# Single rows of an embedding table fetched by two engines in turns, more gathers taken from GpSimd, and a later load of table parts

## The chip, the cores and the metric

The kernel runs on one core of a Trainium2 chip. The metric is the device time of one execution in microseconds (us). The profile is of one execution, and its span is the time between its first and its last recorded instruction.

## The reference

`r_seq` is 1024 x 50 item numbers, `table` 100001 rows of 128 float32, of which row 0 counts as zero.

```python
e = emb_table.at[0].set(0.0)[seq]                 # 1024 x 50 x 128
prefix = jnp.cumsum(e, axis=1)
denom = jnp.minimum(t_idx, lengths)               # t_idx = 1..50
uF = prefix / denom
y = (uF - uF.mean(0)) * rsqrt(uF.var(0) + 1e-5) * gamma + beta   # over the batch, for each step
# for each of the 50 steps, with v = 0 at first:
v = v + (x - v) / 2.0
spike = v >= 1.0
v = v - spike * 1.0
# mean of the spikes over the steps, times the whole table
scores = spikes.mean(0) @ emb.T                   # 1024 x 100001 float32, 409.6 MB
```

## The kernel before

The order of instructions on each engine is that in which the code emits them. Tiles hold the 128 features on the partitions and the 1024 sequences in the columns.

**First stage, a loop over t = 0 to 49.** `gather(t)` fetches the rows of step t into a tile `e` (two buffers): GpSimd (POOL in the profile) issues up to eight indirect DMAs of 128 rows each (line 247). TensorE (PE) transposes the eight blocks and adds them to the running sums `pre0` and `pre1` (line 390), ahead of which `correct` (line 348) takes row 0 out. VectorE (DVE) scales the sums to `uF` (line 401) and takes mean and variance, `bs` and `mv` (lines 402 and 410). ScalarE (ACT) makes the root `r` (line 414), centres `uF` (line 421), scales it to `v` (line 444) and takes `d = v - 1` (line 360); between these VectorE makes the small factors `q` and `a` and the new `v`. `gather(t + 2)` stands behind the transposes of step t, because it writes into the buffer that they read. So GpSimd may be up to two steps ahead of TensorE.

**Rows fetched one by one.** For the eight steps in `BY_SYNC`, GpSimd gathers only seven blocks. The eighth comes from `held_rows`, a tile of four slots of 128 columns. Its 128 rows are fetched one by one by SyncE (SP) in `fetch_singles`: four times a load of 32 byte addresses into registers (line 265) and 32 DMAs of one row of 512 bytes (line 268). The first 128 rows are emitted ahead of the loop, the next 128 at step 11 behind its transposes, and so on.

**Table parts.** SyncE first loads the beginning of the table, 38 parts of 0.5 MB (`fetch`, line 147): four small loads or groups for the first parts, and `AHEAD - 1` = 5 whole groups of six parts (3072 KB each). At step 44 one more load of two parts follows (line 473).

**Second stage.** The counts of spikes are multiplied with the table, part by part (transposes and products on TensorE, lines 176 and 200; copies by VectorE and ScalarE, lines 601 and 603), and SyncE stores the scores (line 209).

**Completion semaphores.** The DMAs of SyncE and ScalarE take eight completion semaphores in turn, in the order of the code, and each DMA waits until the earlier one on its semaphore has landed.

Of the kernel before, what the change touches and what calls it, by code (L numbers as in the profile page):

```python
# [17 lines left out]
U8 = mybir.dt.uint8  # L18
# [3 lines left out]
P = 128  # L22
# [4 lines left out]
BANK = 512  # L27
GROUP = 6
AHEAD = 6
# [3 lines left out]
SHIFT = TWICE + ASIDE  # L33
FURTHER = {5: 1, 6: 2}

BY_SYNC = (11, 17, 22, 28, 33, 38, 43, 48)
AT_ONCE = 32

SPARED = 120
PICKED = range(42, 97, 3)  # L40
# [7 lines left out]
def rec_kernel(  # L48
# [9 lines left out]
    nc = tc.nc  # L58
    B, T = seq.shape
    N, D = table.shape  # L60
    NB = B // P
# [16 lines left out]
    held_rows = const.tile([P, BANK], F32, tag="countB", name="held_rows")  # L78
# [16 lines left out]
    def pair(i):  # L95
        free.append([embp.tile([P, HALF], F32R, tag=f"{x}{i}", name=f"{x}_{i}") for x in ("hi", "lo")])

    def size(q):
        return min(HALF, N - q * HALF)
# [4 lines left out]
    def group(g):  # L104
        at = g if g < AHEAD else AHEAD - 2 + g % 2
        r = rowp.tile([P, GROUP, HALF], F32, tag=f"rows{at}", name=f"rows_{g}")
        for k in range(GROUP):
            rows[g * GROUP + SHIFT + k if g else k + ASIDE * (k >= TWICE)] = r[:, k, :]
        return r
# [19 lines left out]
    def pick(r, q, engine):  # L129
        j = PICKED.index(q)  # L130
        rows_of(r[:SPARED, :], picks, j)
        if j % 2:
            engine.dma_start(out=r[SPARED:, :], in_=runs[q * P + SPARED : (q + 1) * P, :])
            turn_by(TURN)
        else:
            turn_by(4)
            rows_of(r[SPARED:, :], ends, j // 2)
            turn_by(5)

    def fetch(r, k, q, n):  # L140

        engine = nc.sync if q < held else nc.scalar
        n = min(n, parts - q)
        whole = n - (size(q + n - 1) < HALF)
        wide = whole - (whole == n and q + whole - 1 in PICKED)
        if wide:
            engine.dma_start(
                out=r[:, k : k + wide, :],
                in_=table[q * HALF : (q + wide) * HALF, :].rearrange("(q p k) d -> p q (k d)", p=P, k=KQ),
            )  # L150
        if wide < whole:
            pick(r[:, k + wide, :], q + wide, engine)
        if whole < n:
            full, rest = divmod(size(parts - 1), KQ)
            c1 = (parts - 1) * HALF
            r = r[:, k + whole, :]
            if rest:
                at = full - full % 32
                nc.vector.memset(r[at : at + 32, :], 0.0)
                engine.dma_start(  # L160
                    out=r[full : full + 1, : rest * D],
                    in_=table[c1 + full * KQ : N, :].rearrange("(o k) d -> o (k d)", o=1),
                )
            if full:
                engine.dma_start(
                    out=r[:full, :],
                    in_=table[c1 : c1 + full * KQ, :].rearrange("(p k) d -> p (k d)", k=KQ),
                )
# [19 lines left out]
    def prepare(q, pt):  # L188
        turned(q, pt)
        split[q] = hi, lo = free.pop(0)  # L190
        vp, vh, vl = views(q, pt, hi, lo)
        nc.scalar.copy(vh, vp)  # L192
        nc.vector.tensor_tensor(vl, vp, vh.bitcast(F32), ALU.subtract)  # L193
# [18 lines left out]
    with ExitStack() as ph:  # L212
# [21 lines left out]
            rows[TWICE + k] = spare[:, k, :]  # L234
        fetch(spare, 0, TWICE, ASIDE)
        fetch(first, TWICE, SHIFT, GROUP - TWICE)
        for g in range(1, AHEAD):
            fetch(group(g), 0, g * GROUP + SHIFT, GROUP)


# [2 lines left out]

        def gather(t):
            es[t] = gp.tile([P, B], F32, tag="e", name=f"e_{t}")
            for n in range(NB - (t in BY_SYNC)):
                nc.gpsimd.indirect_dma_start(  # L247
                    out=es[t][:, n * P : (n + 1) * P],
                    out_offset=None,
                    in_=table,  # L250
                    in_offset=bass.IndirectOffsetOnAxis(ap=idx[:, n, t : t + 1].bitcast(U32), axis=0),
                )

        byte_rows = table.rearrange("n d -> (n d)").bitcast(U8)
        row_bytes = 4 * D
        starts = ids[:T, :P].bitcast(I32)
        regs = [nc.sync.alloc_register(f"row{k}") for k in range(AT_ONCE)]
        singles = {}

        def fetch_singles(i):  # L260
            t = BY_SYNC[i]
            rows_of = held_rows[:, i % (BANK // P) * P :][:, :P]
            singles[t] = rows_of
            for p0 in range(0, P, AT_ONCE):
                nc.sync.load(regs, starts[t : t + 1, p0 : p0 + AT_ONCE])  # L265
                for k, reg in enumerate(regs):
                    at = nc.sync.snap(reg, donate=True, min_val=0, max_val=(N - 1) * row_bytes)
                    nc.sync.dma_start(  # L268
                        out=rows_of[p0 + k : p0 + k + 1, :].bitcast(U8),
                        in_=byte_rows[bass.ds(at, row_bytes)].rearrange("(o b) -> o b", o=1),  # L270
                    )

        make_identity(nc, ident)
        isz = up.tile([P, NB, P], F32, tag="uF", name="isz")
        rb = up.tile([P, NB, P], F32, tag="uF", name="rb")
        gather(0)

        last_ids = ids[:, P : P + T]
        nc.vector.tensor_copy(last_ids, idx[:, NB - 1, :])
        ips = vp.tile([P, B], F32, tag="v0", name="ips")  # L280
        nc.tensor.transpose(ips[:T, :P], last_ids, ident)
        nc.vector.tensor_scalar_mul(starts, ips[:T, :P], float(row_bytes))
        fetch_singles(0)

        nc.vector.memset(isz, 0.0)
        for u in (0, P // 2):
# [46 lines left out]
        def only(t):  # L333

            k = t % ONLY
            if k == 0:
                n = min(ONLY, T - t)
                nc.vector.tensor_tensor(
                    ls[:, :n, :],
                    r0n.unsqueeze(1).to_broadcast([P, n, D]),  # L340
                    sel[:, t : t + n].unsqueeze(2).to_broadcast([P, n, D]),
                    ALU.mult,
                )
            return ls[:, k, :]
# [12 lines left out]
        def over(t, v):  # L357

            d = lp.tile([P, B], BF16, tag="d", name=f"d_{t}")
            nc.scalar.activation(d, v, AF.Identity, bias=less)  # L360
            return d
# [4 lines left out]
        def spiked(out, cs, v):  # L366
            nc.vector.scalar_tensor_tensor(out, v, V_TH, count[:, cs], ALU.is_ge, ALU.add)
# [12 lines left out]
        correct(0, only(0))  # L380
        l = only(1)
        gather(1)
        for t in range(T):
            last = t == T - 1
# [17 lines left out]
                nc.vector.bn_stats(bs[:, h, :], uF[:, cs])  # L402
            if t + 2 < T:
                gather(t + 2)
            if t in BY_SYNC[:-1]:
                fetch_singles(BY_SYNC.index(t) + 1)
            if not last:
                correct(t + 1, l)
            mv = sp.tile([P, 2], F32, tag="mv", name=f"mv_{t}")
# [33 lines left out]
            def x(vt, cs):  # L443
                nc.scalar.activation(vt, uF[:, cs], AF.Identity, bias=hgb[:, 1:2], scale=a)

            def step(vt, cs):
                nc.vector.scalar_tensor_tensor(vt, negv[:, cs], -0.5, vt, ALU.mult, ALU.add)  # L447

            if not last:
                vt = vp.tile([P, B], F32, tag=f"v{(t + 1) % 2}", name=f"v_{t}")  # L450
                x(vt, whole)
                if t:
                    spiked(count, whole, v)
                step(vt, whole)
                v = vt
                if t == T - 2:
                    spiked(count, whole, v)
                    moved = once.tile([P, P], F32, tag="r0hi", name="moved")
                    nc.vector.tensor_scalar_add(moved, v[:, pieceA], beta2)
                    near = once.tile([P, P], F32, tag="r0", name="near")  # L460
                    nc.vector.scalar_tensor_tensor(near, v[:, pieceA], V_TH, moved, ALU.is_ge, ALU.subtract)
                d = over(t, v)
                if t + 2 < T:
                    l = only(t + 2)

                if t in (T - 8, T - 6):
                    q = (t - T + 8) // 2
                    pair(q)
                    prepare(q, vp.tile([P, HALF], F32, tag="v0", name=f"pt_{q}"))
                    if q == TWICE - 1:  # L470
                        for k in range(TWICE):
                            rows[GROUP + ASIDE + k] = first[:, k, :]
                        nc.sync.dma_start(
                            out=first[:, :TWICE, :],
                            in_=table[(GROUP + ASIDE) * HALF : (GROUP + SHIFT) * HALF, :].rearrange(
                                "(q p k) d -> p q (k d)", p=P, k=KQ
                            ),
                        )

# [64 lines left out]
    for c, W in enumerate(WIDTHS):  # L546
# [38 lines left out]
        for n, q in blockwise:  # L585
# [4 lines left out]
            o = os[n]  # L590
# [27 lines left out]
            if n in (1, 4) and c >= MIDDLE and to_fetch < parts:  # L618
                g, k = divmod(to_fetch - SHIFT, GROUP)
# [26 lines left out]
```

## Time and profile before

| | us |
|---|---|
| three runs | 1845.76, 1851.0, 1854.84 |
| median | 1851.0 |
| profiled execution, its time | 1852.0 |
| its span | 1850.0 |
| first store of scores issued, from the start of the span | 802.8 |
| `r` of steps 0, 1, 2 and 3 | 22.5, 31.1, 49.2, 62.1 |
| `r` of steps 10 and 11 | 140.6, 178.8 |
| `r` of steps 48 and 49 | 789.0, 798.2 |

The mean granted clock of TensorE is 0.763. Over the span PE is busy for 58%, DVE 51%, ACT 36% and POOL 23%, and DMAs move 264 GB/s. These are means over two stages that differ: up to 802.8 us the 50 steps, behind it the products and stores. The times of `r` show how the steps go: most are short, and those in `BY_SYNC`, as step 11, take 30 to 50 us.

### The profile page before, as it was taken

How to read it: one execution, taken by the hardware profiler on the slowest of the kernel's cores; microseconds unless marked ns; L12 is line 12 of the kernel's file. 1: busy time of each engine (PE TensorE's matmuls, PEld its weight loads, DVE VectorE, ACT ScalarE, POOL GpSimd, SP SyncE). 2: the span in 40 equal slices, each digit the busy share in tenths (PEclk: the TensorE clock that was granted, in tenths of full speed). 3: DMA queues.
4: the chain of work that ended last, by engine and by line, in shares of the span. 5: the costliest groups of instructions: out<-in, count | busy, mean ns of one | idle time of the engine just before them, and what ended most of it. 6: DMA issues, size and time to landing. Idle time of an engine off the chain costs nothing.

```text
span 1850.0 us, 14486 instructions
## 1 busy us (share of the span) xinstructions
PE 1070.6 (58%) x4465; PEld 810.4 (44%) x4465; DVE 947.7 (51%) x1128; ACT 674.2 (36%) x698; POOL 429.7 (23%) x459
## 2 busy tenths in 40 slices
PE   3321302120212213088998988878888878888984
PEld 2110201010101112066676766666666666666763
DVE  4653707261524346175566655555555555555652
ACT  2331303130312123054555544444444444444542
POOL 6664716262716254200000000010010010000000
PEclk7555555555555555589999999999889899989998
DMA  9511101010201011069999999999999999999999
GB/s 351 178 44 28 49 15 46 21 48 16 50 14 45 17 41 32 15 266 413 405 422 402 431 421 426 425 427 428 426 427 427 426 427 428 423 422 429 427 428 391
DMA packets 54993, 488.27 MB, mean 264 GB/s; under 512 B 12719, under 2 KB 14000, under 8 KB 33796
## 3 DMA queue, kind: packets, MB, share of 16 engines
q1 hardware_dynamic: 32944, 431.39, 55.4%
q0 software_dynamic: 16560, 35.40, 6.6%
q10 hardware_dynamic: 5412, 20.56, 2.7%
q8 instruction: 35, 0.57, 0.1%
q14 instruction: 42, 0.34, 0.1%
HBM read 77.69 MB, written 409.60 MB: 263 GB/s over the span
## 4 chain that ended last, share of the span: by engine, by line
DMA 33%; PE 15%; DVE 4%; ACT 3%; SPq 3%; issue 3%; ACTq 0%; DVEq 0%
DMA scores<-o 33%; PE po L200 15%; DVE o L601 2%; ACT o L603 2%; SPq L268 2%; DVE pairs L193 1%; ACT pairs L192 1%; PE pt L176 0%; SPq L265 0%; ACT hi L192 0%; DVE lo L193 0%; DVE bs L402 0%; DVE uF L401 0%; DMA held_rows<-in_L_rec_emb_table 0%; ACTq L603 0%
## 5 line engine op out<-in xcount | busy, mean ns | idle before, releaser
L601 DVE TENSOR_SCALAR o<-po 128x1024 f32<-128x1024 f32 (+1 forms) x390 | 467.2, 1214 | 309.6 <-DMA scores<-o 163.7
L603 ACT ACTIVATE o<-po 128x1024 f32<-128x1024 f32 x392 | 393.2, 1025 | 490.7 <-DMA scores<-o 337.2
L247 POOL DMA_INDIRECT e<-in_L_rec_emb_table,idx x392 | 372.9, 951 | 377.2 <-PE pre L390 218.6
L200 PE MATMUL po<-pairs,countB 128*128 128x512 f32 (+1 forms) x1120 | 289.9, 404 | 47.8 <-ACT o L603 47.6
L200 PE MATMUL po<-pairs,countC 128*128 128x512 f32 (+1 forms) x840 | 243.9, 438 | 62.3 <-ACT o L603 55.4
L401 DVE SCALAR_TENSOR_TENSOR uF<-rlen,pre 128x512 f32<-128x512 f32 x100 | 67.9, 679 | 399.0 <-PE pre L390 317.2
L200 PEld LDWEIGHTS po<-pairs,countB 128*128 128x128 f32 x1120 | 208.3, 191 | 110.9 <-ACT o L603 64.9
L200 PEld LDWEIGHTS po<-pairs,countC 128*128 128x128 f32 x840 | 169.8, 210 | 115.9 <-ACT o L603 66.0
L348 PE MATMUL pre<-zT,ls 128*128 128x512 f32 x100 | 78.5, 787 | 227.3 <-DVE uF L401 136.7
L390 PE MATMUL pre<-ident,held_rows 128*128 128x128 f32 x8 | 3.6, 447 | 349.2 <-DMA held_rows<-in_L_rec_emb_table 349.2
L414 ACT ACTIVATE r<-mv,eps 128x1 f32<-128x1 f32 x50 | 14.8, 295 | 509.2 <-DVE mv L410 406.3
L122 POOL DMA_INDIRECT rows<-in_L_rec_emb_table,picks x19 | 18.6, 981 | 685.2 <-PE pt L176 681.9
L390 PEld LDWEIGHTS pre<-ident,held_rows 128*128 128x128 f32 x8 | 1.5, 183 | 351.7 <-issue 351.7
L348 PEld LDWEIGHTS pre<-zT,ls 128*128 128x128 f32 x100 | 29.4, 295 | 267.4 <-DVE uF L401 159.3
L193 DVE TENSOR_TENSOR pairs<-pt,pairs 128x1024 fp32r<-128x1024 f32 x70 | 85.3, 1218 | 98.0 <-ACT pairs L192 97.1
L390 PE MATMUL pre<-ident,e 128*128 128x128 f32 x392 | 101.3, 422 | 19.2 <-DMA e<-in_L_rec_emb_table,idx 12.7
L176 PE MATMUL pt<-ident,rows 128*128 128x128 f32 (+1 forms) x768 | 104.9, 282 | 9.3 <-DVE v L447 5.0
L176 PEld LDWEIGHTS pt<-ident,rows 128*128 128x128 f32 (+1 forms) x768 | 94.3, 147 | 26.3 <-issue 10.8
L390 PEld LDWEIGHTS pre<-ident,e 128*128 128x128 f32 x392 | 81.6, 219 | 37.4 <-DMA e<-in_L_rec_emb_table,idx 18.9
L200 PE MATMUL po<-hi,countB 128*128 128x512 f32 x208 | 84.8, 408 | 10.8 <-ACT o L603 9.2
L192 ACT CAST pairs<-pt 128x1024 fp32r<-128x1024 f32 x70 | 70.0, 1012 | 39.2 <-PE pt L176 39.2
L200 PE MATMUL po<-lo,countB 128*128 128x512 f32 x208 | 83.3, 401 | 0.0
(99 smaller groups left out, 1110.1 us busy)
## 6 DMA issues: line engine op xcount, KB each, us to landing
scores<-o SPq DMA_DIRECT2D x96, 3072.0 KB
scores<-o SPq DMA_DIRECT2D x32, 1536.0 KB
scores<-o SPq DMA_DIRECT2D x29, 1024.0 KB
scores<-o SPq DMA_DIRECT2D x8, 2896.5 KB
rows<-in_L_rec_emb_table ACTq DMA_DIRECT2D x19, 1024.0 KB
held_rows<-in_L_rec_emb_table SPq DMA_DIRECT2D x1024, 0.5 KB
rows<-in_L_rec_emb_table SPq DMA_DIRECT2D x5, 3072.0 KB
e<-in_L_rec_emb_table,idx POOLq DMA_INDIRECT x392
```

The source lines that it names most:

```text
L122: nc.gpsimd.indirect_dma_start(out=r, out_offset=None, in_=runs, in_offset=bass.IndirectOffsetOnAxis(ap=which[: r.shape[0], j : j + 1].bit ...
L176: nc.tensor.transpose(pt[:, k0 : k0 + pw], r[:pw, k0 : k0 + D], ident[:pw, :pw])
L192: nc.scalar.copy(vh, vp)
L193: nc.vector.tensor_tensor(vl, vp, vh.bitcast(F32), ALU.subtract)
L200: nc.tensor.matmul(po[:, :kw], lhsT=counts[n], rhs=part[:, k0 : k0 + kw], start=j == 0, stop=j == 1,)
L247: nc.gpsimd.indirect_dma_start(out=es[t][:, n * P : (n + 1) * P], out_offset=None, in_=table, in_offset=bass.IndirectOffsetOnAxis(ap=idx[: ...
L268: nc.sync.dma_start(out=rows_of[p0 + k : p0 + k + 1, :].bitcast(U8), in_=byte_rows[bass.ds(at, row_bytes)].rearrange("(o b) -> o b", o=1),)
L348: nc.tensor.matmul(pre[h], lhsT=l, rhs=zT[:, h * BANK : (h + 1) * BANK], start=t == 0, stop=False, skip_group_check=True,)
L390: nc.tensor.matmul(pre[h][:, k : k + P], lhsT=singles[t] if h * BANK + k + P == B and t in singles else e[:, h * BANK + k : h * BANK + k + P],
L401: nc.vector.scalar_tensor_tensor(uF[:, cs], rlen[:, cs], 1.0 / (t + 1), pre[h], ALU.max, ALU.mult)
L601: nc.vector.tensor_scalar_mul(o[:, h0 : h0 + hw], po[:, :hw], 1.0 / T)
L603: nc.scalar.mul(o[:, h0 : h0 + hw], po[:, :hw], 1.0 / T)
```

## The change

The single rows now serve eleven steps, `APART` = 7, 11, 15, ..., 47, instead of eight. They are fetched in 44 portions of 32 rows. A portion is emitted at the end of each step from `STARTED` = 1 on, so in steps 1 to 44: SyncE loads 22 addresses and fetches 22 rows, ScalarE loads 10 and fetches 10, the two emitted in turns (SyncE, ScalarE, SyncE, ...) until ScalarE has its ten. Of the groups of table parts that SyncE loaded first, those from `EARLY` = 2 on (four groups) are loaded behind the last portion. In the changed file the loads of addresses are lines 274 and 275, the single rows 265, gathers 249, table parts 149, `r` 421, `uF` 428, `v` 451, `d` 369, the reload 480 and the stores 211.

```diff
-BY_SYNC = (11, 17, 22, 28, 33, 38, 43, 48)
-AT_ONCE = 32
+APART = tuple(range(7, 48, 4))
+STARTED = 1
+SYNC_ROWS, OWN_ROWS = 22, 10
+EARLY = 2
...
-        for g in range(1, AHEAD):
+        for g in range(1, EARLY):
             fetch(group(g), 0, g * GROUP + SHIFT, GROUP)
...
-            for n in range(NB - (t in BY_SYNC)):
+            for n in range(NB - (t in APART)):
                 nc.gpsimd.indirect_dma_start(
...
-        regs = [nc.sync.alloc_register(f"row{k}") for k in range(AT_ONCE)]
+        sync_regs = [nc.sync.alloc_register(f"row{k}") for k in range(SYNC_ROWS)]
+        own_regs = [nc.scalar.alloc_register(f"own{k}") for k in range(OWN_ROWS)]
...
-        def fetch_singles(i):
...
+        def fetch_row(engine, reg, row):
+            at = engine.snap(reg, donate=True, min_val=0, max_val=(N - 1) * row_bytes)
+            engine.dma_start(
+                out=row.bitcast(U8),
+                in_=byte_rows[bass.ds(at, row_bytes)].rearrange("(o b) -> o b", o=1),
+            )
+
+        def fetch_some(i, p0):
+            t = APART[i]
+            rows_of = singles[t] = held_rows[:, i % (BANK // P) * P :][:, :P]
+            p1 = p0 + SYNC_ROWS
+            nc.sync.load(sync_regs, starts[t : t + 1, p0:p1])
+            nc.scalar.load(own_regs, starts[t : t + 1, p1 : p1 + OWN_ROWS])
+            for k, reg in enumerate(sync_regs):
+                fetch_row(nc.sync, reg, rows_of[p0 + k : p0 + k + 1, :])
+                if k < OWN_ROWS:
+                    fetch_row(nc.scalar, own_regs[k], rows_of[p1 + k : p1 + k + 1, :])
+
+        todo = [(i, p0) for i in range(len(APART)) for p0 in range(0, P, SYNC_ROWS + OWN_ROWS)]
...
-        fetch_singles(0)
...
-            if t in BY_SYNC[:-1]:
-                fetch_singles(BY_SYNC.index(t) + 1)
...
+                if t >= STARTED and todo:
+                    fetch_some(*todo.pop(0))
+                    if not todo:
+                        for g in range(EARLY, AHEAD):
+                            fetch(group(g), 0, g * GROUP + SHIFT, GROUP)
```

In the order of instructions a row names the line, the operation, and the tile written and read. `rows` and `spare` are table parts, `ids` the byte addresses, `held_rows` the single rows. SyncE's opening was this before:

```order
L147 DMA rows_106<-in_L_rec_emb_table 128x4x1024
L147 DMA rows_111<-in_L_rec_emb_table 128x6x1024
L147 DMA rows_113<-in_L_rec_emb_table 128x6x1024
L147 DMA rows_115<-in_L_rec_emb_table 128x6x1024
L147 DMA rows_117<-in_L_rec_emb_table 128x6x1024
L147 DMA rows_119<-in_L_rec_emb_table 128x6x1024
L265 TENSOR_LOAD ids
L268 DMA held_rows<-in_L_rec_emb_table 1x512 x32
```

And it is this with the change:

```order
L149 DMA rows_106<-in_L_rec_emb_table 128x2x1024
L149 DMA spare<-in_L_rec_emb_table 128x2x1024
L149 DMA rows_106<-in_L_rec_emb_table 128x4x1024
L149 DMA rows_111<-in_L_rec_emb_table 128x6x1024
L274 TENSOR_LOAD ids
L265 DMA held_rows<-in_L_rec_emb_table 1x512 x22
```

The single rows now stand behind one group instead of five, and go in portions of 22. The end of SyncE's first stage, with the first store (`scores`), was this before:

```order
L265 TENSOR_LOAD ids
L268 DMA held_rows<-in_L_rec_emb_table 1x512 x32
L473 DMA rows_106<-in_L_rec_emb_table 128x2x1024
L209 DMA scores<-o_0_3455 128x512 x2
L209 DMA scores<-o_1_3456 128x512 x2
```

And with the change:

```order
L480 DMA rows_106<-in_L_rec_emb_table 128x2x1024
L274 TENSOR_LOAD ids
L265 DMA held_rows<-in_L_rec_emb_table 1x512 x22
L149 DMA rows_3652<-in_L_rec_emb_table 128x6x1024
L149 DMA rows_3654<-in_L_rec_emb_table 128x6x1024
L149 DMA rows_3656<-in_L_rec_emb_table 128x6x1024
L149 DMA rows_3658<-in_L_rec_emb_table 128x6x1024
L211 DMA scores<-o_0_3892 128x512 x2
```

Four groups have come between the last single row and the first store. ScalarE's queue at the end of one early step and the beginning of the next was this before:

```order
L444 ACTIVATE v_372<-uF_336,hgb,a_368 128x1024
L360 ACTIVATE d_375<-v_372,less 128x1024
L414 ACTIVATE r_404<-mv_402,eps 128x1
L421 ACTIVATE uF_377<-uF_377,mv_402 128x1024
L444 ACTIVATE v_414<-uF_377,hgb,a_410 128x1024
```

And with the change:

```order
L451 ACTIVATE v_274<-uF_237,hgb,a_270 128x1024
L369 ACTIVATE d_278<-v_274,less 128x1024
L275 TENSOR_LOAD ids
L265 DMA held_rows<-in_L_rec_emb_table 1x512 x10
L421 ACTIVATE r_341<-mv_339,eps 128x1
```

A load of ten addresses and ten rows have come between `d` of one step and `r` of the next.

More of the change, by code (lines that the diff above doesn't have):

```diff
@@ L256, in rec_kernel @@
         starts = ids[:T, :P].bitcast(I32)
-        regs = [nc.sync.alloc_register(f"row{k}") for k in range(AT_ONCE)]
+        sync_regs = [nc.sync.alloc_register(f"row{k}") for k in range(SYNC_ROWS)]
+        own_regs = [nc.scalar.alloc_register(f"own{k}") for k in range(OWN_ROWS)]
         singles = {}
-        def fetch_singles(i):
[L261 to L271, printed above, removed]
+        def fetch_row(engine, reg, row):
[15 more added lines that the diff above has]
+        todo = [(i, p0) for i in range(len(APART)) for p0 in range(0, P, SYNC_ROWS + OWN_ROWS)]
         make_identity(nc, ident)
```

## The prediction

> **What bounds the kernel now.** I read the page first, then the busy time of three stretches (windows), then the waits up to the first store, and last the order in time of SyncE (SP), GpSimd (POOL) and ScalarE (ACT) in single stretches. The stretches show two stages:
>
> ```profile
> 0.00:46.00 46.00, 16.40 (x48) 9.30 (x48) 20.75 (x44) 11.09 (x12) 31.97 (x38) 0.77 0.95 351
> 64.00:785.00 721.00, 151.84 (x455) 98.82 (x455) 320.53 (x544) 165.09 (x180) 332.41 (x353) 0.51 0.13 33
> 802.80:1850.00 1047.20, 885.09 (x3899) 688.57 (x3897) 581.45 (x491) 486.58 (x491) 54.99 (x58) 0.95 1.00 421
> ```
>
> The columns are PE, PEld, DVE, ACT and POOL busy, then the granted clock, the share of the DMA engines and GB/s. From the first store at 802.8 to the end the DMA engines are full (1.00, 421 GB/s): 1047.2 us that the change leaves alone. Before it, from 64 to 785, no engine is half busy. The waits up to 802.8 say what the 50 steps wait for:
>
> ```profile
> ACT r L414 <- DVE mv L410: 406.3, 21, 50.6
> PE pre L390 <- DMA held_rows<-in_L_rec_emb_table: 349.2, 8, 50.5
> POOL e L247 <- PE pre L390: 218.6, 10, 36.7
> ```
>
> Eight times TensorE stands for some 44 us in front of the transpose of `held_rows`, the rows that SyncE fetches one by one; ScalarE and GpSimd then stand behind it. So SyncE's issuing sets the first stage, and its pace is to be read in time:
>
> ```profile
> 64.44 720.92 SPq L268 DMA_DIRECT2D held_rows<-in_L_rec_emb_table  x1017
> 164.92 10.28 SPq L268 DMA_DIRECT2D held_rows<-in_L_rec_emb_table  x32
> 180.81 20.43 SPq L268 DMA_DIRECT2D held_rows<-in_L_rec_emb_table  x21
> 222.18 20.41 SPq L268 DMA_DIRECT2D held_rows<-in_L_rec_emb_table  x9
> ...
> L247 POOL DMA_INDIRECT e<-in_L_rec_emb_table,idx x16 | 15.5, 971 | 26.4 <-PE pre L390 21.8 <-issue 4.6
> ...
> L247 POOL DMA_INDIRECT e<-in_L_rec_emb_table,idx x392 | 372.9, 951 | 377.2 <-PE pre L390 218.6
> ...
> 772.79 2.18 SPq L265
> ```
>
> Columns: start, duration, instruction and count. 1017 rows take 720.92 us without a gap, but at three paces. Between 165 and 175 no gather runs: 32 rows in 10.28 us, 0.32 us each. From 181 to 201 a fresh run of 16 gathers is on (the POOL row is of that stretch): 21 rows in 20.43 us. From 222 to 243 the gathers have been running for 20 us: 9 rows in 20.41 us, 2.3 us each. SyncE is slow while GpSimd gathers, whatever the reason. The row of all 392 gathers (from the page) gives 951 ns for one, and in the row above it 4.6 us of "issue" lie in 15 gaps: 0.30 us to the next. The last row is the load of 32 addresses into registers (from the chain), 2.18 us for each 32 rows.
>
> A check of this reading: the 353 gathers of the second stretch are 353 x 1.25 = 441 us. At the mean of both gathering paces (30 rows in 40.84 us, 0.73 per us) that is 324 rows. The other 693 go at 32 rows in 10.28 + 2.18 us (2.57 per us): 270 us. The sum is 711 against 720.92; the missing 10 us I put to the slow end of each run of gathers. The table parts come first on SyncE:
>
> ```profile
> 4.08 35.58 SPq L147 DMA_DIRECT2D rows<-in_L_rec_emb_table  x6
> 41.96 23.68 SPq L268 DMA_DIRECT2D held_rows<-in_L_rec_emb_table  x11
> ...
> 779.97 5.39 SPq L268 DMA_DIRECT2D held_rows<-in_L_rec_emb_table  x17
> 785.48 0.41 SPq L473 DMA_DIRECT2D rows<-in_L_rec_emb_table  x1
> 802.80 25.24 SPq L209 DMA_DIRECT2D scores<-o  x16
> ...
> 785.13 1.27 DMA held_rows<-in_L_rec_emb_table
> ```
>
> The last single row is issued at 785.1 and lands 1.27 us later; steps 48 and 49 and the first store follow by 802.8, 17.7 us behind it.
>
> **The change part by part.** GpSimd: 11 gathers leave instead of 8, three gathers fewer, 3.75 us of an engine that waits 218.6 us for TensorE. Worth nothing; the cover is the wait of TensorE for the rows.
>
> SyncE: 44 portions of 22 rows are 968 rows instead of 1024, with 44 loads instead of 32. A load of 22 registers costs between 1.50 us (22/32 of 2.18) and 2.18 us, so a portion takes 22 x 0.32 = 7.06 us and the load: 2.38 to 2.57 rows per us in quiet time; I take 2.47, the middle.
>
> The opening: 14 of the 38 parts are loaded first, 7.3 MB, which at 351 GB/s is done by some 21 us; rows can start then, not at 41.96. The opening's first and last of 32 gathers, `r` of step 1, and the moved bytes by slices of 1.15 us and the size of a group:
>
> ```profile
> 3.58 1.14 POOL L247 DMA_INDIRECT e<-in_L_rec_emb_table,idx  x1 [2.25 <-DMA idx<-in_r_seq]
> ...
> 43.35 0.94 POOL L247 DMA_INDIRECT e<-in_L_rec_emb_table,idx  x1 [0.30 <-issue]
> ...
> 31.10 0.29 ACT L414 ACTIVATE r<-mv,eps 128x1 f32<-128x1 f32 x1 [3.60 <-DVE bs L402]
> ...
> GB/s 0 33 164 41 176 349 395 427 403 385 406 385 381 392 388 385 388 381 413 385 388 385 388 388 381 392 385 385 385 403 392 388 385 385 385 385 392 381 392 388
> ...
> rows<-in_L_rec_emb_table SPq DMA_DIRECT2D x5, 3072.0 KB
> ```
>
> Until 44 us GpSimd makes its first 32 gathers without a long stop, and beside long gathering SyncE did 9 rows in 20.4 us: 10 rows by 44. After that ScalarE stands in step 1 for its own rows (below), GpSimd with it, and SyncE has quiet time; I give it 28 rows more by 65 us, about half of what 0.32 us each would allow. So 38 rows at 65 us, where before there were 7 (1024 less 1017) at 64.4. Bounds: 10 to 60 rows, 11 us less gain or 9 more.
>
> The rest: 968 - 38 = 930 rows. Gathers after the first 32: 389 - 32 = 357, 446 us. TensorE now needs single rows every fourth step, before every fifth or sixth, so the runs of gathers are a little shorter and their fresh half counts more; I take 0.77 rows per us between 0.44 (all deep) and 1.03 (all fresh), nearest to the calibrated 0.73: 343 rows. The remaining 587 rows at 2.47 take 237 us. With the 10 us for the ends of the runs, the last row is issued at 65 + 446 + 237 + 10 = 758 us (before: 785).
>
> ScalarE: 440 rows and 44 loads stand in its queue behind `d` and ahead of the next `r`. Between these it has, in a step that waits for nothing:
>
> ```profile
> 190.65 1.11 ACT L360 ACTIVATE d<-v,less 128x1024 bf16<-128x1024 f32 x1 [1.30 <-issue]
> 193.52 0.29 ACT L414 ACTIVATE r<-mv,eps 128x1 f32<-128x1 f32 x1 [1.76 <-DVE mv L410]
> ...
> 198.00 1.11 ACT L360 ACTIVATE d<-v,less 128x1024 bf16<-128x1024 f32 x1 [1.30 <-issue]
> ```
>
> A step is 198.00 - 190.65 = 7.35 us with 1.76 us of slack before `r`. Ten rows at SyncE's quiet 0.32 us with a load of at most 2.18 us are 5.4 us, 3.6 more than the slack: 11 us for a step. All 44 would take 484 us, and SyncE needs 693 us (758 - 65) for its portions: beside it, nothing on the path. What waits behind these rows is `r`, then VectorE's reciprocal and TensorE two steps on. No ScalarE row stands in the trace; the ends are 0.32 us (SyncE in quiet) and 2.3 us (SyncE beside long gathering). I take the first, since the rows above lie within a run of gathers and ScalarE starts them on time there, while SyncE crawls.
>
> New waits: rows of both engines share eight completion semaphores in turn, so a row waits for the landing of the one eight issues earlier, on either engine. The landing is 1.27 us and a portion leaves it room; between 0 and 44 x 1.27 = 56 us, I take 0, as SyncE's own wait for landings is small:
>
> ```profile
> SPq L268 <- DMA held_rows<-in_L_rec_emb_table: 5.7, 12, 0.8
> ```
>
> The end of the stage: four groups of six parts, 4 x 3072 KB = 12.6 MB, now stand on SyncE behind its last row and ahead of the first store. At the 380 to 400 GB/s that the opening shows once it is full (its first slices pull the mean down to 351) this is 31 to 36 us; I take 33. Steps 47 to 49 hide part of it: 17.7 + 7.35 = 25 us. So the first store moves at 758 + 33 = 791 instead of 802.8.
>
> Sum: 802.8 - 791 = 12 us gained. The profiled execution has a span of 1850.0 and a time of 1852, one us over the median 1851.0 of the three runs. 1852 - 12 = **1840 us**. By its own bounds (loads, opening, pace in gathers within 0.1, waits) this case lies between 1815 and 1860. A change under 0.5% (9 us) can't be told from none here.
>
> **A rule weighed.** The rows show issuing at 0.32 to 2.3 us a row. The Trainium skill, "DMA: Bandwidth & Descriptors", section "Issuing engines are not separate DMA queues", says that starting DMAs on several engines saves only the sequencer's time to start them, and that this is usually small against the DMA itself. For these rows the trace disagrees with "usually small": the issue is the whole cost, and a landing is 1.27 us.
>
> **Rivals.** First, slower: ScalarE's rows crawl beside the gathers as SyncE's do. Place: the rows between `d` and `r`, which begin 4 us into a run of gathers. Of the ten, some three go by the gathers' end (0.73 per us), the rest in quiet time, so ScalarE reaches `r` some 16 us after the last `r` instead of 11; and since the shared semaphores then make SyncE wait for ScalarE's rows within the quiet time, the portions come one behind the other: 16 us and the landing, 17.3 us a step. 44 x 17.3 + 31 (step 1's `r`) = 792, with 33 = 825 for the first store: +22 us, and with each landing waited for twice (56 us more) +78. Middle: 1900. It decides when ScalarE needs over 15.8 us a step (693/44). For it: the slowness hits two engines, since VectorE also waited 71.9 us in all for TensorE's signals in that stage,
>
> ```profile
> DVE uF L401 <- remote: 71.9, 13, 8.7
> ```
>
> with the last TensorE record long past; against it: ScalarE and VectorE themselves start on time. The same skill page, section "Rules for kernel authors", says that small transfers below 64 KB are mostly overhead and should be merged; by that, 384 more transfers (1408 for 1024) for three gathers speak for this rival.
>
> Second, faster: ScalarE's waits part the gathers into runs of one step, each run finds SyncE fresh. The fresh run gives about 17 of its 21 rows in its first half, so 22 rows and a load need 10 us of gathers and (22 + 7 - 17)/3.1 = 3.9 us of quiet, 13.9 us a step: 65 + 43 x 13.9 = 663, first store 696, time 1745. Against it: GpSimd may run two steps ahead, and did so in nearly every run of this trace.
>
> Third, no change: loads at 2.18 us, 10 rows at 65 us and 5 us of landings take the 12 us back: 1850 to 1858. That is also where the change would end if splitting the issue did nothing but drop three gathers.
>
> **How the numbers follow.** Forecast 0.46 (1815 to 1847), slower by ScalarE's rows 0.28 (1860 to 1930), no change 0.17, runs of one step 0.09. The 80% range leaves out the fastest rival and the upper part of the slow one: 1805 to 1915. Faster by over 0.5% (below 1841.7): 0.33 of the forecast's 0.46 and 0.09, 0.42; slower (above 1860.3): 0.28, and 0.09 of the other two; same: the remaining 0.21.
>
> **What would show it.** Right: SyncE's last single row near 758, SyncE never idle from 25 us on; the wait of TensorE for `held_rows` cut from 349 us, and the time showing instead as ScalarE standing ahead of `held_rows` rows; its rows 0.3 to 0.5 us each when nothing holds them, during gathers too; first store near 791, right behind the groups' loads; 1047 us from there. Wrong: ScalarE rows of over 1 us with their registers' moves slow as well (first rival); gathers in runs of eight with pauses of 4 us (second); a first store further than 36 us from the last row, or a second stage that grew.

## The result, and the profile after

The changed kernel took 1828.92 us in the median of six runs (1825.92 to 1834.64), the kernel before 1849.97 us in six (1845.76 to 1855.39): ratio 0.9888, interval 0.9862 to 0.9913, faster by 21 us where 12 were forecast. The profiled execution took 1834.64 us, the longest of the six; its span is 1832.7 us against 1850.0 before.

Busy time in three stretches of the changed kernel (columns as before):

```profile
0.00:46.00 46.00, 14.88 (x47) 9.64 (x47) 19.48 (x42) 11.09 (x12) 32.04 (x38) 1.00 0.61 212
64.00:750.00 686.00, 143.06 (x445) 96.01 (x445) 316.00 (x536) 162.93 (x178) 328.05 (x348) 0.78 0.14 36
780.02:1832.70 1052.68, 888.97 (x3899) 690.28 (x3897) 581.78 (x491) 486.83 (x491) 55.16 (x58) 0.94 1.00 422
```

The first store stands at 780.0 instead of 802.8, 22.8 us earlier. The second stage takes 1052.7 us instead of 1047.2, 5.5 us longer. The difference is the 17.3 us between the spans. The rest of the 21 lies in the choice of executions: the one profiled was 5.7 us over its median, that of before 2.0 over its own, and 17.3 + 5.7 - 2.0 = 21.0.

SyncE in order of time, first up to 65 us, then its end:

```profile
7.67 56.56 SPq L265 DMA_DIRECT2D held_rows<-in_L_rec_emb_table  x32
...
747.94 7.72 SPq L265 DMA_DIRECT2D held_rows<-in_L_rec_emb_table  x22
755.72 11.54 SPq L149 DMA_DIRECT2D rows<-in_L_rec_emb_table  x4
780.02 50.12 SPq L211 DMA_DIRECT2D scores<-o  x23
```

By 65 us SyncE has issued 32 single rows (38 were forecast, 7 before). The last one is issued at 755.4 us (758 forecast). Behind it stand the four groups. Their issue ends at 755.72 + 11.54 = 767.3, and the first store goes at 780.0, not at 791.

What the first stage waits for, up to 800 us:

```profile
ACT r L421 <- DMA held_rows<-in_L_rec_emb_table: 305.3, 34, 28.2
PE pre L399 <- DMA held_rows<-in_L_rec_emb_table: 273.1, 11, 36.4
POOL e L249 <- PE pre L399: 218.3, 15, 22.1
```

TensorE waits 273 us for single rows instead of 349, in eleven places instead of eight; as forecast, ScalarE now stands ahead of `r` for single rows (305 us). In three of these 34 waits, such as the one up to 444.0, its own rows had been issued some 11 us before `r`, which then stood behind TensorE: 32 us in all. GpSimd waits as long for TensorE as before (218.3 against 218.6 us).

ScalarE's rows (ACTq) in one cycle of four steps:

```profile
462.30 7.08 ACTq L265 DMA_DIRECT2D held_rows<-in_L_rec_emb_table  x10
469.43 0.29 ACT L421 ACTIVATE r<-mv,eps 128x1 f32<-128x1 f32 x1 [8.93 <-DMA held_rows<-in_L_rec_emb_table]
475.83 6.81 ACTq L265 DMA_DIRECT2D held_rows<-in_L_rec_emb_table  x9
...
492.87 3.41 ACTq L265 DMA_DIRECT2D held_rows<-in_L_rec_emb_table  x10
```

At 492.87, with no gather running, ten rows take 3.41 us, the forecast price. At 462 and 476, late in runs of gathers, nine or ten take 7 us, and single instructions of them 0.7 us: they are slowed too, and by more than I had taken. One early portion is of another kind. Its rows, and the instructions of both engines beside it (`MOVE` sets the address of a row; count, then shortest, median and longest in ns), from 61 to 86 us:

```profile
61.78 23.86 ACTq L265 DMA_DIRECT2D held_rows<-in_L_rec_emb_table  x10
...
L265 SPq MOVE held_rows<-in_L_rec_emb_table x14: 3/690/1387, 61.4 to 84.2; - x14
...
L265 ACTq DMA_DIRECT2D held_rows<-in_L_rec_emb_table x10: 217/228/462, 61.8 to 85.4; - x10
```

Ten rows take 23.86 us, though none of ScalarE's DMAs took over 0.46 us, while SyncE's address moves took 0.69 us in the median. So ScalarE itself is not slow there. It stands between its rows, and by the order of the completion semaphores what it stands for is the landing of SyncE's slow rows; that is read from these times, and no run parts the two.

### The profile page after: what moved, and what is told of

It reads as the page before. It is cut to its first block, busy times and chain, and to the rows that moved or that the text cites. A ratio compares the mean times of both kernels' runs of the same rounds, so it can differ in the third digit from the quotient of the medians.

```text
span 1832.7 us, 15332 instructions
## 1 busy us (share of the span) xinstructions
PE 1068.6 (58%) x4465; PEld 812.2 (44%) x4465; DVE 949.4 (52%) x1128; ACT 674.6 (37%) x698; POOL 426.6 (23%) x456
## 4 chain that ended last, share of the span: by engine, by line
DMA 36%; PE 13%; DVE 5%; ACT 3%; issue 2%; SPq 2%; ACTq 0%; DVEq 0%
DMA scores<-o 36%; PE po L202 12%; DVE o L614 3%; ACT o L616 2%; SPq L265 2%; DVE pairs L195 1%; ACT pairs L194 1%; PE pt L178 0%; DMA rows<-in_L_rec_emb_table 0%; ACT hi L194 0%; DMA held_rows<-in_L_rec_emb_table 0%; DVE bs L411 0%; DVE uF L410 0%; DVE lo L195 0%; DVE v L454 0%
## 5 line engine op out<-in xcount | busy, mean ns | idle before, releaser
L249 POOL DMA_INDIRECT e<-in_L_rec_emb_table,idx x389 | 369.6, 950 | 365.5 <-PE pre L399 218.3
L434 DVE RECIPROCAL r<-r 128x1 f32<-128x1 f32 x50 | 8.1, 162 | 178.5 <-issue 111.7
L399 PE MATMUL pre<-ident,e 128*128 128x128 f32 x389 | 94.5, 418 | 3.9 <-DMA e<-in_L_rec_emb_table,idx 2.2
L194 ACT CAST pairs<-pt 128x1024 fp32r<-128x1024 f32 x70 | 70.0, 1012 | 41.2 <-PE pt L178 41.2
```

The lines of the kernel that those rows point to most:

```text
L249: nc.gpsimd.indirect_dma_start(out=es[t][:, n * P : (n + 1) * P], out_offset=None, in_=table, in_offset=bass.IndirectOffsetOnAxis(ap=idx[: ...
L399: nc.tensor.matmul(pre[h][:, k : k + P], lhsT=singles[t] if h * BANK + k + P == B and t in singles else e[:, h * BANK + k : h * BANK + k + P],
```

## The experiments

The experiments ran on several chips, and these are of two kinds. On some, that of the result among them, the kernel before takes 1828 to 1850 us, as in the first profile; I call their rows slow. On the others it takes 1552 us, and a single row costs less than 0.35 us even beside gathers (425.9 us for 1024 rows, less 32 loads of some 2.2 us). Each chip was met in one session only, so whether it is the chip or the hour is not shown. Which kind a run met was chance, so some questions were asked several times. Ratios are against the kernel before on the same chip and in the same session.

| run | rows | before, us | this, us | ratio |
|---|---|---|---|---|
| after_2 | slow | 1828.4 | 1815.4 | 0.9955 (0.9923 to 0.9988) |
| parts_first_2 | slow | 1828.4 | 1825.5 | 0.9993 (0.9968 to 1.0018) |
| no_rows_2 | slow | 1828.4 | 1623.9 | 0.8889 (0.8838 to 0.8941) |
| eight_steps | slow | 1847.1 | 1695.5 | 0.9194 (0.9148 to 0.9241) |
| after_3 | not slow | 1551.4 | 1665.3 | 1.0727 (1.0709 to 1.0745) |
| parts_first | not slow | 1552.3 | 1694.7 | 1.0912 (1.0893 to 1.0931) |
| sync_alone | not slow | 1552.3 | 1663.7 | 1.0717 (1.0699 to 1.0735) |
| sixteen | not slow | 1552.3 | 1610.5 | 1.0373 (1.0356 to 1.0391) |
| no_rows | not slow | 1552.3 | 1560.8 | 1.0057 (1.0040 to 1.0074) |
| four_ahead | not slow | 1552.4 | 1564.7 | 1.0078 (1.0061 to 1.0095) |
| parts_last | not slow | 1552.4 | 1555.0 | 1.0018 (1.0008 to 1.0027) |
| no_gathers | not slow | 1552.4 | 1532.1 | one run |

**The change again, and its base.** after_2 and after_3 are the changed kernel, before_2 the kernel before.

> The changed kernel again. If rows beside gathers crawl (2.3 us), as in the two profiles at the start, it is 1 per cent faster than the kernel before, 0.989. If they go at 0.32 us throughout, as in the first four experiments, where the kernel before takes 1552 us, the change can only add: ScalarE's rows ahead of r and the waits of SyncE and ScalarE for each other's rows. There the version with all parts first took 1695 us; an opening 20 us earlier for SyncE and 0 to 6 us for late loads make some 1675 to 1690 us, a ratio of 1.08 to 1.09.

> The kernel before again, for its profile. Where it takes 1552 us, single rows beside a run of gathers take 0.32 us each and none over 0.5; the first stage is then bounded by GpSimd, 392 x 1.25 = 490 us, and the first store comes near 504 us. Where it takes 1850 us, rows beside gathers take up to 2.3 us again and the first store comes near 803 us.

> The changed kernel, as the base for the two versions beside it. Where rows crawl beside gathers: 1810 to 1830 us, 0.99 of the kernel before. Where they do not, and the kernel before takes 1552 us: ScalarE's rows ahead of r and the two engines' waits for each other's rows set the steps at some 13 us; the version with all parts first took 1695 us, and the late load is worth 10 to 17 us: 1675 to 1690 us.

Where rows are slow the medians now differ by 13 us, and the ratio over all runs is half a per cent (before_2 alone: 1830.1 us). On a chip where rows are not slow the change costs 114 us, 7 per cent; I had expected 1675 to 1690 us there and got 1665. SyncE's rows in the kernel before (before_2) and in the changed kernel (after_2), on the same chip:

```profile
41.21 722.06 SPq L268 DMA_DIRECT2D held_rows<-in_L_rec_emb_table  x1024
...
780.61 49.65 SPq L209 DMA_DIRECT2D scores<-o  x25
```

```profile
7.32 716.74 SPq L265 DMA_DIRECT2D held_rows<-in_L_rec_emb_table  x946
...
726.60 7.46 SPq L265 DMA_DIRECT2D held_rows<-in_L_rec_emb_table  x22
734.11 11.68 SPq L149 DMA_DIRECT2D rows<-in_L_rec_emb_table  x4
757.65 70.96 SPq L211 DMA_DIRECT2D scores<-o  x31
```

The first store moves by 23.0 us here, as in the first pair of profiles (22.8), and the spans differ by 17.0 us (17.3 there). The granted clock does not carry this: in the first stage it was 0.51 before and 0.78 with the change in the first pair, and 0.51 in both profiles of this one.

**All table parts first** (parts_first, parts_first_2) takes the late load out of the change:

```diff
-EARLY = 2
+EARLY = AHEAD
```

> The changed kernel with all table parts loaded at the start, as in the kernel before. In the changed kernel SyncE issued few rows before 49 us, so an early start gains next to nothing; the loads at the end were hidden up to the first store and then cost the second stage some 5 us (1052.7 us against 1047.2). By that the first store stays at 780 +- 5 us and the time falls by 0 to 6 us, to 1823 to 1830 us. By the prediction's sum: the opening's 28 rows (11 us) are lost and 33 us of loads in front of the first store go, with 25 us of steps behind the last row: 791 - 33 + 25 + 11 = 794 us, some 14 us slower than the changed kernel, 1843 us.

> The changed kernel with all table parts loaded at the start. Where rows crawl: the first store stays within 5 us of the changed kernel's 780 and the second stage is 5 us shorter, 1823 to 1830 us, if the late loads were hidden and the early start gained nothing; 1843 us by the prediction's sum. Where they do not crawl: 1695 us again.

SyncE in parts_first_2 with its wait in the opening, and the second stage of it and of after_2:

```profile
SPq L265 <- DMA held_rows<-in_L_rec_emb_table: 18.0, 1, 18.0
...
64.21 676.77 SPq L265 DMA_DIRECT2D held_rows<-in_L_rec_emb_table  x946
...
743.51 7.53 SPq L265 DMA_DIRECT2D held_rows<-in_L_rec_emb_table  x22
775.87 52.39 SPq L211 DMA_DIRECT2D scores<-o  x27
...
775.87:1823.30 1047.43, 882.96 (x3899) 686.16 (x3897) 581.40 (x491) 486.79 (x491) 55.14 (x58) 0.95 1.00 421
```

```profile
757.65:1811.10 1053.45, 889.05 (x3898) 690.19 (x3896) 582.93 (x492) 487.04 (x491) 54.99 (x58) 0.94 1.00 422
```

Three things are to be read here. With no load behind the rows the first store still comes 775.87 - (743.51 + 7.53) = 24.8 us behind them, against 757.65 - (726.60 + 7.46) = 23.6 us with the loads. So the loads delay the first store by nothing; they cost the second stage 1053.45 - 1047.43 = 6.0 us. Second, the early opening is worth 751.0 - 734.1 = 16.9 us at the last row. Third, without the late load the change is worth nothing that can be measured (0.9993). Its last row comes 12 us before that of the kernel before (763.3 in before_2), but it serves step 47 instead of 48, one step of 7.35 us more behind it, and the first store gains only 780.6 - 775.9 = 4.7 us; the medians 3 us. Two things lie in this that I had not taken apart: the 968 rows take 686.8 us against 722.1 for 1024, 35 us less, but the first of them goes at 64.2 us instead of 41.2, because SyncE stands 18.0 us for the landing of another single row. So the 16.9 us of the early opening hold this wait as well as the table parts. My expectation of no loss without the late load (1823 to 1830 us) was met at 1825.5, but for a wrong reason: it had given the opening nothing, and compared with the changed kernel (1815.4) the loss is 10 us. The prediction's sum (14 us slower) was nearer.

**No rows at all** (no_rows, no_rows_2): all 400 gathers on GpSimd, parts first.

```diff
-APART = tuple(range(7, 48, 4))
+APART = ()
-EARLY = 2
+EARLY = AHEAD
```

> All 400 gathers on GpSimd, no single rows, all table parts loaded first. If the fetching of single rows is what sets the first stage, it falls to GpSimd's pace of eight gathers, 8 x 1.25 = 10.0 us a step: 50 steps, first store near 520 to 560 us, time near 1590 us. The rival: rows are a relief, because TensorE's signals also come late while gathers run without a stop. Steps 2 and 3 in the opening of the kernel before, beside unbroken gathers, took 18 and 13 us; at 13 to 18 us a step the first store comes at 670 to 920 us and the time lies between 1720 and 1970 us, no gain at the upper end.

> All gathers on GpSimd, no single rows. Where the kernel before takes 1850 us: if single rows and nothing else are what gathers slow down, steps go at GpSimd's 10 us as they did in the first run of this kernel, and the time is again 1555 to 1570 us, 0.84 of the kernel before. If the gathers slow everything that signals, TensorE's signals above all, steps take 13 to 18 us, 1720 to 1970 us. Where the kernel before takes 1552 us: 1561 us again, 1.006.

Where rows are not slow this runs at GpSimd's 10.0 us a step and takes 1560.8 us; the kernel before is 9 us faster there, so its single rows did what they were for. Where they are slow it takes 1623.9 us, 204 us less than the kernel before, and beats both kernels. It lies between the two expectations (1555 to 1570, and 1720 or more). The gathers alone still make signals late there; from 60 to 500 us:

```profile
DVE uF L410 <- remote: 125.4, 19, 10.0
...
POOL e L249 <- remote: 42.5, 13, 5.1
```

These are waits for a signal whose sender the view does not name. In the traces TensorE's last record is long past then; in the first run of this kernel, on a chip without slow rows, the view has no row with "remote".

**Is it the gathers?** no_gathers fetches blocks for steps 0 and 1 alone and uses them again; parts_last (below) has all its gathers.

```diff
+            if t > 1:
+                es[t] = kept[t % 2]
+                return
```

> The kernel before with gathers for steps 0 and 1 alone; later steps use their blocks again, so it leaves out the gathering of 376 blocks. Single rows stay as they are: 1024, all on SyncE. If the gathers are what slows SyncE, all rows go at 32 in 10.28 + 2.18 us: 32 x 12.46 = 399 us, last row at 441, first store near 460 and time near 1508 us. If SyncE slows itself (its queue, its registers, landings), rows of 1 to 2.3 us stay and the first stage stays near 780 us.

SyncE's rows in no_gathers, then in parts_last, both on the same chip without slow rows:

```profile
38.97 425.92 SPq L271 DMA_DIRECT2D held_rows<-in_L_rec_emb_table  x1024
```

```profile
7.81 425.91 SPq L268 DMA_DIRECT2D held_rows<-in_L_rec_emb_table  x1024
```

1024 rows take 425.9 us with gathers or without. On the chips with slow rows they take 722 to 743 us, and the rows beside no gather keep 0.32 us there. That rows are slow there while gathers run is what the traces show in time; that the gathers are the cause is not shown. The direct trial would be no_gathers on such a chip, and no run of it met one (its repeat took 1530.0 us on another chip without slow rows). What sets the two kinds of chip apart is open too.

**Late parts in the kernel before** (parts_last):

```diff
-        for g in range(1, AHEAD):
+        for g in range(1, 2):
             fetch(group(g), 0, g * GROUP + SHIFT, GROUP)
...
+                        for g in range(2, AHEAD):
+                            fetch(group(g), 0, g * GROUP + SHIFT, GROUP)
```

> The kernel before with one edit: four groups of table parts load behind the reload of step 44 instead of first, the rest unchanged (eight steps with rows by SyncE alone). In the changed kernel the late load was worth 17 us at the first store and cost 5 us in the second stage. Here the last rows serve step 48, so the loads have 18 us of steps beside them instead of 25 and cost the second stage some 12 us. If the early start is worth 17 us again: 1828 - 17 + 12 = 1823 us, ratio 0.997; if it is worth little without portions, because the first 128 rows are wanted only at step 11: 1828 + 12 = 1840 us, 1.006. Where rows do not crawl: 1552 + 12 to 15 us, 1.01.

It ran twice, both times on chips without slow rows: 1555.0 and 1554.6 us, 1.002 of the kernel before, less than the 1.01 expected. Whether the late load alone would give the kernel before its 10 us where rows are slow stays open.

**The split of the rows** (sync_alone: 32 and 0; sixteen: 16 and 16).

```diff
-SYNC_ROWS, OWN_ROWS = 22, 10
+SYNC_ROWS, OWN_ROWS = 32, 0
```

> The changed kernel with all 32 rows of a portion on SyncE and none on ScalarE (1408 rows and 44 loads of 32 addresses). If SyncE's issuing sets the stage and ScalarE's rows cost nothing on the path, the last row comes 440 rows later at 32 rows in 10.28 + 2.18 us: 171 us later, time near 2000 us. If instead ScalarE's rows are what the steps wait for (they stand ahead of r for 305 us in the changed kernel), taking them away gives back as much as it costs: 1800 to 1860 us.

> The changed kernel with all 32 rows of a portion on SyncE. Where rows crawl beside gathers: 1986 us, 1.09 of the kernel before, if SyncE's issuing alone sets the stage (440 rows at 32 in 12.46 us, 171 us more); 1815 to 1860 us if the engines' waits for each other cost what ScalarE's share saves, as it did where rows do not crawl (1664 us against 1665). Where they do not crawl: 1664 us again.

> The changed kernel with 16 rows of a portion on SyncE and 16 on ScalarE instead of 22 and 10. If SyncE sets the pace, it has 44 x 6 = 264 rows less at 0.32 us, 84 us, and loads of 16 addresses instead of 22, some 0.4 us each, 18 us: the first store near 680 us and the time near 1730 us. If ScalarE's rows crawl beside gathers and hold r, six more of them a step at 0.32 to 2.1 us cost 2 to 12 us a step on the path: 1900 us or more. Between the two, a balance: 1790 to 1860 us.

All ran on chips without slow rows; sync_alone four times, 1663.7 to 1664.6 us each. SyncE's rows in sync_alone_4, in after_3, and its wait for landings in after_3 from 42 to 760 us:

```profile
578.27 10.56 SPq L265 DMA_DIRECT2D held_rows<-in_L_rec_emb_table  x32
```

```profile
7.59 568.07 SPq L265 DMA_DIRECT2D held_rows<-in_L_rec_emb_table  x946
...
578.19 8.07 SPq L265 DMA_DIRECT2D held_rows<-in_L_rec_emb_table  x22
...
SPq L265 <- DMA held_rows<-in_L_rec_emb_table: 146.3, 99, 5.4
```

Both end at the same time. With 32 rows a portion SyncE is simply full: 44 portions of 32 rows at 425.92/32 = 13.3 us are 586 us. With 22 it has a third less to issue, but stands 146 us for landings of single rows; in sync_alone_4 the same view has no such wait. So I put it to rows that ScalarE issues late, between its steps, and that SyncE waits for by the shared semaphores. There they give back the whole of ScalarE's share. In sixteen ScalarE stands for its own rows in 44 of the steps, and SyncE is done with 688 of its 704 rows by 377 us:

```profile
6.72 370.44 SPq L265 DMA_DIRECT2D held_rows<-in_L_rec_emb_table  x688
...
ACT r L421 <- DMA held_rows<-in_L_rec_emb_table: 273.5, 44, 10.4
```

ScalarE has become the bound there, and 1610 us is better than either, though still 58 us behind the kernel before. What ScalarE's share is worth where rows are slow was not measured.

**Eight steps** keeps everything of the change but the number of steps with single rows:

```diff
-APART = tuple(range(7, 48, 4))
+APART = (11, 17, 22, 28, 33, 38, 43, 48)
```

> The changed kernel with single rows for the eight steps of the kernel before (32 portions, in steps 1 to 32), the rest as changed: 22 + 10 rows in turns, late loads. Where rows do not crawl, SyncE's portions take 568 us / 43 = 13 us each with its waits; 32 of them end near 430 us, ahead of the steps that want them, so GpSimd's 392 gathers bind again: first store near 510 us, 1555 to 1570 us against 1665 with eleven steps. If the two engines' waits for each other stretch the steps themselves, it stays above 1600 us. Where rows crawl: 264 rows less for SyncE at 0.32 us and 12 loads less at 1.9 us, 107 us, against three gathers more, 4 us: some 1715 us against 1815 with eleven steps; if ScalarE's rows hold the steps there, 1780 us or more.

It met a chip with slow rows: 1695.5 us, 0.919. SyncE in order of time:

```profile
8.19 604.68 SPq L265 DMA_DIRECT2D held_rows<-in_L_rec_emb_table  x704
612.92 11.75 SPq L149 DMA_DIRECT2D rows<-in_L_rec_emb_table  x4
624.79 7.31 SPq L480 DMA_DIRECT2D rows<-in_L_rec_emb_table  x1
632.20 194.38 SPq L211 DMA_DIRECT2D scores<-o  x64
```

704 rows end at 612.9 instead of 968 at 755 (the chip of the result), 143 us earlier; 107 were expected from the quiet price, so the rows left out cost 0.54 us each, more than 0.32, with their loads. SyncE issues rows throughout in both (its waits for their landings are 13 and 12 us in all), so its issuing sets the first stage on such a chip: fewer rows, shorter stage. ScalarE's rows fell too, from 440 to 320, and no run parts what each of the two was worth. The second stage takes 1691.9 - 632.2 = 1059.7 us, 7.0 more than in the changed kernel: the groups have only 632.2 - 612.9 = 19.3 us ahead of the first store instead of 24.3, and the reload at line 480 now stands behind them.

**Four buffers** for gathers without single rows (four_ahead; tile `room` is that of the last group, loaded behind step 49):

```diff
-            es[t] = gp.tile([P, B], F32, tag="e", name=f"e_{t}")
+            es[t] = room[:, t % 4, :]
...
-            if t + 2 < T:
-                gather(t + 2)
+            if t + 4 < T:
+                gather(t + 4)
+            if last:
+                fetch(group(AHEAD - 1), 0, (AHEAD - 1) * GROUP + SHIFT, GROUP)
```

> No single rows, and four buffers for gathers instead of two (in the room of the last group of table parts, which is loaded behind the last step), so that GpSimd may run four steps ahead. Where signals crawl beside gathers, the version with two buffers took 1624 us, 11.2 us a step, because GpSimd waited for TensorE's late signals after each 32 gathers. If only that wait costs, GpSimd's 10.0 us a step is reached: first store near 515 us, time 1562 to 1575 us. If longer runs make all signals later still, the steps do not follow and the time is 1620 us or more. Where nothing crawls: 1561 us as with two buffers, and up to 8 us for the last group's load.

It ran only where signals are not late, and there it took 1564.7 us, as expected. Whether it brings no_rows below 1624 us elsewhere is open.

## Why the prediction was right or wrong, point by point

- **What bounds the stage: right.** SyncE's issuing does: on chips with slow rows 1024, 968 and 704 rows end near 763 to 785, 734 to 755 and 613 us.
- **The opening: right, its worth too small.** 32 rows at 65 us where 38 were forecast. parts_first_2 gives its worth, 16.9 us, where I had 28 rows or 11 us; that run also holds SyncE's wait of 18.0 us for the landing of a single row, which the changed kernel does not have.
- **The last row: right.** 755.4 for 758 us. It is a sum of terms that lean both ways. I took SyncE's wait for shared semaphores as 0; it was 11.6 us in the changed kernel (42 to 760 us; 23.9 in after_2):

```profile
SPq L265 <- DMA held_rows<-in_L_rec_emb_table: 11.6, 14, 3.6
```

- **ScalarE's price: half right.** 0.34 us a row in quiet (ten in 3.41 us), 0.7 us late in runs of gathers. In the cycle shown, `r` came 11.5, 13.9 and 13.5 us after the last one, instead of 11; step 3, behind the portion of 23.86 us, took 33.6. The slower rival's mechanism was there, but mostly below the 15.8 us a step from which it decides.
- **The end of the stage: the step that failed.** "The first store moves at 758 + 33" set the whole transfer of four groups in front of the first store. Only their issue stands there, 11.54 us, and the first store waits for step 49 anyway: it came 24.6 us behind the last row, the three steps' own time, of which I had counted 25 us myself, but as cover for a part alone. The moved bytes from 750 to 810 us in the changed kernel, 1.5 us a number, show the transfer under the last steps, and the engines still full when the stores begin:

```profile
GB/s 1 2 1 7 44 358 415 410 421 421 410 410 418 404 410 412 410 404 412 412 410 412 404 412 418 376 376 403 403 393 423 423 426 410 421 399 426 431 410 421
```

The DMA engines are full from 758 us on. 12.6 MB at 411 GB/s take 31 us by estimate, to 788; the stores begin at 780 and share the engines for 8 us, and the second stage is 5.5 us longer (6.0 between parts_first_2 and after_2, which differ in the late load alone). So 33 us should have been 24.6 at the store and 5.5 behind it. At the first store the forecast misses 11.0 us: 8.4 from this term and 2.6 from the last row. The second stage, taken as untouched, takes 5.5 back; that it grew is a sign that I had named.
- **The second failure is in what I sized against.** The 12 us stood against one profiled execution, and 1840 us lie only 10 us below the median of six runs (1849.97); the measured 21 is between medians, 17.3 between profiled spans. So of the 9 us that the forecast was short, 2.6 are the last row's, 2.9 (8.4 - 5.5) the end of the stage's, and 3.7 (5.7 - 2.0) lie in which executions were profiled, which no term foresaw. In the second pair (before_2, after_2) the spans differ by 17.0 us again, but the medians by 13. The profiles agree, and the medians leave the size of this change open by some 8 us.
- **The rivals.** That dropping three gathers and splitting the issue does nothing by itself holds where it was tried: 0.9993 without the late load. The faster rival (runs of one step) did not come: GpSimd stopped 15 times for TensorE in 50 steps (10 before), for as long in all as before. The change came out slower by 7 per cent where rows are not slow. There SyncE alone would be full with the 1408 rows (sync_alone), and the shared semaphores, which I had put at 0, give back what ScalarE's share saves: SyncE's waits for landings are 146.3 us (after_3), against 11.6 and 23.9 where rows are slow.

## What to carry to other kernels

When an issuing queue is the bound, count what is left in it: the change moved 1408 rows to serve eleven steps and left SyncE 968 of its 1024, so it gained little beside its earlier start; serving eight steps with the same split left 704 and gained 8 per cent. A load that is issued behind the last urgent transfer cost, in this kernel, the bandwidth that it still took when the next stage began (5.5 to 6.0 us), not its length (31 us). Two engines whose transfers share completion semaphores in turn can be held to the pace of the one that issues later, as SyncE was in after_3.

## What the runs showed of the hardware

- The same kernel takes 1552 or 1828 to 1850 us by the chip or the session, and the sign of this change depends on it (0.989 and 0.996 against 1.073). A kernel that is tuned on one kind of chip is not tuned for the other; no_rows is within 1 per cent of the best on one and 11 per cent better than the kernel before on the other.
- Where rows are slow, it is not SyncE alone: ScalarE's rows take twice as long late in runs of gathers (7.08 us for ten against 3.41), part of which can be waits for SyncE's rows, and with no rows at all VectorE still stands 125.4 us for late signals.
